# Loads and folded weights at the start of a one-core hybrid kernel: another order on the queues

## The chip, the cores and the metric

The kernel runs on one core of a Trainium2 chip. The metric is the device time of the whole program in microseconds (us). TensorE (PE) multiplies matrices, its weight loads are listed as PEld; VectorE is DVE, ScalarE is ACT, GpSimd is POOL. SP computes nothing here; it issues DMAs. ACT and POOL issue DMAs too. An engine works through its own instructions in order, and an instruction that issues a DMA is one of them.

## What is computed

The reference is three layers on one image of 256 channels and 64 x 64 pixels, which are also seen as 4096 tokens of 256 values; `_gn` is a group norm over groups of 8 channels and all pixels, `_ln_t` a layer norm per token.

```python
x = x + _L0_conv_ref(_gn(x), ...)
t = _to_tokens(x)
t = t + _L1_attn_ref(_ln_t(t), ...)
t = t + _L1_ffn_ref(_ln_t(t), ...)
x = _from_tokens(t, x)
...
# layer 0: 8 heads of 32, boxes of 64, 32 and 16 pixels around each pixel
q, k = sigmoid(einsum(x, Wq)), sigmoid(einsum(x, Wk))
v = v / max(norm(v), 1e-12)
Ik, Ikv = _integral(k), _integral(einsum('bfhw,bghw->bfghw', k, v))
for w in WINDOWS:
    wk, wkv = _box(Ik, Hh // w, Hh, Ww), _box(Ikv, Hh // w, Hh, Ww)
    outs.append(einsum('bdhw,bdfhw->bfhw', q, wkv) / (einsum('bdhw,bdhw->bhw', q, wk)[:, None] + 1e-06))
return einsum('bchw,oc->bohw', concatenate(outs, axis=1), Wout) + bout[None, :, None, None]
...
# layer 1: causal attention over 4096 tokens, then a small MLP
A = softmax(where(causal, einsum('bqd,bkd->bqk', q, k), MASK_FILL) / D ** 0.5)
out = _layernorm(einsum('bqk,bkd->bqd', A, v) + x, g_ln, beta_ln)
return _layernorm(relu(out @ W1.T + b1) @ W2.T + b2, g_lnff, beta_lnff)
...
# layer 2: two of eight experts, chosen from the mean over the tokens
h = gelu(einsum('nd,edf->enf', xf, W1) + b1[:, None, :])
y = einsum('enf,efd->end', h, W2) + b2[:, None, :]
return _layer_norm(einsum('ne,end->nd', w_dense, y) + x, gamma, beta)
```

Layer 1 needs Wq and Wk only as a product. For that the kernel folds them once: mm = Wq^T Wk, a vector mb from Wk and bq, one more column of the value weights from Wq and bk, and one number from bq and bk.

## The kernel before, in words

`conv_attn_hybrid` calls `window_attention` (layer 0), `causal_attention` (layer 1) and `experts` (layer 2). The change touches the start of layer 0 and the order of some DMAs within it.

At the start of `window_attention`, `load(m)` fetches chunk m of x, 1024 pixels, as two DMAs of 512 KB: channels 0 to 127 by SP, 128 to 255 by ACT (L202). All four chunks are asked for at once; the fourth lies in the buffer `vh`, which is not needed until later. ACT then issues six tables of masks (L212). `first(psum)` is `folded` (L716 on): it loads Wq, Wk, bq, bk, Wv, bv on ACT's queue into buffers of its own, transposes Wq and Wk on PE (L736), copies them out on DVE (L737), multiplies (L748, L753, L758, L765), and stores the four results `fold` to DRAM by SP (L771), from where `Causal.load` (L813) gets them back at the end of layer 0. After it, SP is given the 32 loads of the tokens, `t` (L217, 128 KB each), and POOL that of bout (`bo`, L219). POOL loads three slices of layer 0's weights (L305) and Wout (`wo`, L309).

The group norm: DVE takes `bn_stats` of each half of each chunk (16 in all, L261) and two aggregates (L262); PE multiplies the means by `groups` (L264), DVE forms `d2` (L268 to L270), PE multiplies again (L272), ACT takes the square root (L274), DVE the reciprocal (L275).

`window_heads` runs twice, for heads 0 to 3 (`hg` 0) and 4 to 7 (`hg` 1). Its first stage is a loop over four chunks: `normalise(m + 1)` on DVE (L610), `project` (L517: keys, then queries; ACT's sigmoids L520, L522), `values` (L540, copied by ACT L543; at its end SP stores v to DRAM, four DMAs, L558), then at m = 0 everything in the list `late`, `block_sums`, and `turned` (L573). `fetch(m)` brings v back in another order (L565, two DMAs per chunk). For `hg` 1 `normalise` loads its chunk of x anew (L202).

The second stage goes through lists of window parts: `push` fills four PSUM buffers by PE (L349, L358), and ACT and DVE empty them (L327, L329, five of eight on ACT); `add` multiplies with v (L391). Six PSUM buffers turn in a ring. Where a group of columns is complete, `store` has ACT copy the sum (L402) and issue its DMA to DRAM, `oscratch` (L403); later SP brings it back as `ov` (L667). POOL builds running sums and boxes, then adds bout to the tokens (L652). `convolve` (L505) multiplies by Wout and adds to the tokens.

The order of the work: PE and POOL are in the order of the program text inside `window_heads` (`manual_schedule`); the other engines, SP among them, are put in order by a scheduler that works from costs of its own. At the start of `window_attention` PE is scheduled too. The built program keeps eight completion counters for the DMAs that SP and ACT issue, and hands them round from DMA to DMA. A DMA waits, on the engine that issues it, until the one before it on its counter has landed.

Of the kernel before, what the change touches and what calls it, by code (L numbers as in the profile page):

```python
# [152 lines left out]
@with_exitstack  # L153
def conv_attn_hybrid(ctx: ExitStack, tc: tile.TileContext, a, out):
    nc = tc.nc

    const = ctx.enter_context(tc.tile_pool(name="const", bufs=1))
    ident = const.tile([P, P], F32, name="ident")
    make_identity(nc, ident)
    eps5 = const.tile([P, 1], F32, name="eps5")  # L160
    nc.vector.memset(eps5, 1e-5)

    tok = ctx.enter_context(tc.tile_pool(name="tok", bufs=1))
    t = tok.tile([P, NT, D], F32, name="t")

    dram = ctx.enter_context(tc.tile_pool(name="folded", bufs=1, space=bass.MemoryType.DRAM))
    low = ctx.enter_context(tc.tile_pool(name="low", bufs=1))
    iks = ctx.enter_context(tc.tile_pool(name="iks", bufs=1, reuse_waits="tile"))
    causal = Causal(tc, a, t, ident, eps5, low, iks)
    window_attention(tc, a, t, eps5, ident, causal, lambda psum: folded(tc, dram, psum, a, ident))  # L170
    big = ctx.enter_context(tc.tile_pool(name="l12big", bufs=1, reuse_waits="tile"))
    keep = ctx.enter_context(tc.tile_pool(name="l12keep", bufs=1, reuse_waits="tile"))
    given = Given(nc, a, keep, causal)
    x2 = causal_attention(tc, t, ident, eps5, causal, big, given)
    experts(tc, a, t, out, ident, eps5, given, x2)


def window_attention(tc, a, t, eps5, ident, causal, first):
# [5 lines left out]
    with ExitStack() as ctx:  # L184
# [21 lines left out]
        vh = causal.vh  # L206
        raws = [load(m) for m in range(3)]
        raws.append(load(3, vh.rearrange("p j e -> p (j e)")[:, 0:2048].rearrange("p (c n) -> p c n", c=DC)))
        tables = []
        for i, o in enumerate(window_tables()):  # L210
            s = w.tile(list(o.shape), BF16, name=f"table{i}")
            nc.scalar.dma_start(out=s, in_=a[f"mask{i}"])  # L212
# [37 lines left out]
        pt = psum()  # L250
        wide = sm.tile([P, 4, 32], F32, name="wide", bufs=1)
        nc.vector.tensor_copy(wide, sums.unsqueeze(1).to_broadcast([P, 4, 32]))
        nc.tensor.transpose(pt[:, 0:P], wide.rearrange("p w j -> p (w j)"), ident)
        nc.vector.tensor_copy(spreadh, pt[:, 0:P])


        mv = sm.tile([P, DC, 2], F32, name="mv")
        for c in range(DC):
# [3 lines left out]
            nc.vector.bn_aggr(out=mv[:, c, :], in_=st)  # L262
        pm = psum()
        nc.tensor.matmul(pm[:, 0:DC], lhsT=groups, rhs=mv[:, :, 0], start=True, stop=True)  # L264
        gm = w.tile([P, DC], F32, name="gm")
        nc.vector.tensor_copy(gm, pm[:, 0:DC])
        d2 = sm.tile([P, DC], F32, name="d2")
        nc.vector.tensor_sub(d2, mv[:, :, 0], gm)  # L268
        nc.vector.tensor_mul(d2, d2, d2)
        nc.vector.tensor_add(d2, d2, mv[:, :, 1])  # L270
        pv = psum()
        nc.tensor.matmul(pv[:, 0:DC], lhsT=groups, rhs=d2, start=True, stop=True)  # L272
        rs = w.tile([P, DC], F32, name="rs")
        nc.scalar.activation(rs, pv[:, 0:DC], AF.Sqrt, bias=eps5)  # L274
        nc.vector.reciprocal(rs, rs)  # L275
# [19 lines left out]
def window_heads(tc, a, t, ident, hg, norm, raws, load, psum, pools, tables, consts, late, causal):  # L295
# [417 lines left out]
BIG = NT - 20  # L713


def folded(tc, dram, psum, a, ident):  # L716


    nc = tc.nc
    with ExitStack() as tmp:  # L720
        s = tmp.enter_context(tc.tile_pool(name="foldsm", bufs=1, side="right"))
        mm = s.tile([P, DC, D], F32, name="mm")
        mb = s.tile([P, DC], F32, name="mb")
        wvu = s.tile([P, DC, D + 2], F32, name="wvu")
        nc.gpsimd.memset(wvu[:, :, 0:1], 0.0)
        bvc = s.tile([P, D + 2], F32, name="bvc")
        nc.gpsimd.memset(bvc[:, 0:1], 1.0)
        wT = {}
        for name in ("Wq", "Wk"):
            src = s.tile([P, DC, D], F32, name=f"f{name}")  # L730
            nc.scalar.dma_start(out=src, in_=a["L1_" + name].rearrange("(c p) e -> p c e", p=P))
            dst = s.tile([P, DC, D], F32, name=f"t{name}")
            for e in range(DC):
                pt = psum()[:, 0:D]
                for c in range(DC):
                    nc.tensor.transpose(pt[:, c * P : (c + 1) * P], src[:, c, e * P : (e + 1) * P], ident)  # L736
                nc.vector.tensor_copy(dst[:, e, :], pt)  # L737
            wT[name] = dst
        col = {}
        for name in ("bq", "bk"):  # L740
            col[name] = s.tile([P, DC], F32, name=f"f{name}")
            nc.scalar.dma_start(out=col[name], in_=a["L1_" + name].rearrange("(c p) -> p c", p=P))
        nc.scalar.dma_start(out=wvu[:, :, 1 : D + 1], in_=a["L1_Wv"].rearrange("(c p) e -> p c e", p=P))
        nc.scalar.dma_start(out=bvc[:, 1 : D + 1], in_=a["L1_bv"].partition_broadcast(P))
        for c in range(DC):
            pm = psum()[:, 0:D]
            for e in range(DC):
                nc.tensor.matmul(pm, lhsT=wT["Wq"][:, e, c * P : (c + 1) * P], rhs=wT["Wk"][:, e, :],  # L748
                                 start=(e == 0), stop=(e == DC - 1))
            nc.vector.tensor_copy(mm[:, c, :], pm)  # L750
            pb = psum()[:, 0:D]
            for e in range(DC):
                nc.tensor.matmul(pb[:, 0:1], lhsT=wT["Wk"][:, e, c * P : (c + 1) * P], rhs=col["bq"][:, e : e + 1],  # L753
                                 start=(e == 0), stop=(e == DC - 1))
            nc.vector.tensor_copy(mb[:, c : c + 1], pb[:, 0:1])
            pb = psum()[:, 0:D]
            for e in range(DC):
                nc.tensor.matmul(pb[:, 0:1], lhsT=wT["Wq"][:, e, c * P : (c + 1) * P], rhs=col["bk"][:, e : e + 1],  # L758
                                 start=(e == 0), stop=(e == DC - 1))
            nc.vector.tensor_copy(wvu[:, c, D + 1 :], pb[:, 0:1])  # L760
        bqs = s.tile([P, DC, P], F32, name="bqs")
        nc.vector.tensor_copy(bqs, col["bq"].unsqueeze(2).to_broadcast([P, DC, P]))
        pb = psum()[:, 0:D]
        for e in range(DC):
            nc.tensor.matmul(pb[:, 0:1], lhsT=bqs[:, e, :], rhs=col["bk"][:, e : e + 1],  # L765
                             start=(e == 0), stop=(e == DC - 1))
        nc.vector.tensor_copy(bvc[:, D + 1 :], pb[:, 0:1])
        out = []
        for src in (mm, mb, wvu, bvc):
            d = dram.tile(list(src.shape), F32, name=f"fold{len(out)}")  # L770
            nc.sync.dma_start(out=d, in_=src)  # L771
            out.append(d)
    return out


class Causal:
# [554 lines left out]
```

## Time and profile before

| what | value |
|---|---|
| three timed runs, median | 1993.42 us (1993.35 to 1994.79) |
| the profiled execution's own time | 1994.53 us |
| its span | 1992.8 us |
| mean granted TensorE clock | 0.982 |
| PE busy | 1859.6 us (93%), 20326 instructions |
| DVE, ACT, POOL busy | 1000.5, 777.4, 431.8 us |
| DMA over the span | 53.34 MB, mean 27 GB/s |

The busy row of an engine gives one digit for each of 40 equal slices of the span. A line of the order of time gives start, length, engine, source line, operation, output and input, shapes, how many were merged, and in brackets the idle time before it and what ended that. An engine name with a q (SPq, ACTq) is the engine's queue of issues. A line of waits gives who waited, on what, for how long in total, how often, and the longest. The lines themselves stand in the prediction.

### The profile page before, as it was taken

The numbers are of one execution on the slowest core, as the hardware profiler recorded it, in microseconds if no ns is written. First come the engines' busy times: TensorE is split into PE (matmuls) and PEld (weight loads), VectorE is DVE, ScalarE is ACT, GpSimd is POOL, SyncE is SP. The second block draws the span as 40 slices with busy tenths as digits, with TensorE's granted clock in tenths as the row PEclk, the third lists the DMA queues.
The fourth block names the chain that finished last, engine by engine and source line by source line (L and its number), as shares of the span: only waits on it lengthen the run. The fifth ranks groups of instructions, "written<-read, shape, count | busy, mean of one in ns | idle before, by whom it ended". The sixth has DMA issues, their size and how long they took to land.

```text
span 1992.8 us, 46271 instructions
## 1 busy us (share of the span) xinstructions
PE 1859.6 (93%) x20326; PEld 1218.4 (61%) x20326; DVE 1000.5 (50%) x2190; ACT 777.4 (39%) x1331; POOL 431.8 (22%) x709
## 2 busy tenths in 40 slices
PE   4999999999999999999999999999999999879998
PEld 2655565555665555555575656665666666657777
DVE  4644555544554565555663444554553655443343
ACT  1566444444456644444414233233333234223322
POOL 1384323232155123333110000000000000031220
PEclk9999999999999999999999999999999999879999
DMA  7211100000331100000100000000000000010000
GB/s 242 82 52 45 29 13 18 13 18 12 104 92 40 45 18 18 13 13 13 50 2 0 1 0 1 0 1 0 1 0 1 0 1 0 1 43 22 21 22 22
DMA packets 66890, 53.34 MB, mean 27 GB/s; under 512 B 37568, under 2 KB 56792, under 8 KB 66688
## 3 DMA queue, kind: packets, MB, share of 16 engines
q1 hardware_dynamic: 57296, 31.87, 5.8%
q10 hardware_dynamic: 8128, 14.67, 2.1%
q0 software_dynamic: 1264, 3.84, 0.6%
q8 instruction: 159, 2.61, 0.6%
q14 instruction: 43, 0.35, 0.1%
HBM read 32.93 MB, written 17.44 MB: 25 GB/s over the span
## 4 chain that ended last, share of the span: by engine, by line
PE 42%; DVE 6%; ACT 3%; issue 1%; POOL 0%; ACTq 0%; DVEq 0%; POOLq 0%
PE po L1001 11%; PE pa L957 10%; PE ph L1265 6%; PE py L1285 6%; PE pt L987 2%; PE pm L1058 1%; PE acc L391 1%; PE pm L1068 1%; DVE lnst L704 1%; PE ps L505 1%; DVE sT L990 1%; PE ps L358 1%; DVE nbs L965 1%; PE pm L916 1%; ACT s L970 1%
## 5 line engine op out<-in xcount | busy, mean ns | idle before, releaser
L327 ACT ACTIVATE pm<-ps 128x512 f32<-128x512 f32 (+19 forms) x734 | 362.4, 558 | 348.4 <-issue 194.1
L329 DVE TENSOR_SCALAR pm<-ps 128x512 f32<-128x512 f32 (+23 forms) x442 | 267.6, 636 | 315.7 <-PE ps L358 234.5
L391 PE MATMUL acc<-pm,vh 128*32 128x248 f32 (+22 forms) x3424 | 218.5, 356 | 16.8 <-DVE pm L329 16.7
L358 PE MATMUL ps<-q,kh 32*128 32x248 f32 (+23 forms) x3424 | 204.8, 354 | 0.0
L957 PE MATMUL pa<-k,qT 128*128 128x512 f32 (+3 forms) x416 | 180.2, 574 | 7.1 <-ACT qT L918 5.6
L349 PE MATMUL ps<-table,table 32*128 32x192 bf16 (+19 forms) x2512 | 143.1, 261 | 24.4 <-ACT rn L477 8.4
L990 DVE COPY sT<-pt 128x512 f32<-128x512 f32 (+3 forms) x144 | 92.7, 644 | 142.9 <-PE pt L987 142.7
L391 PEld LDWEIGHTS acc<-pm,vh 128*32 128x32 f32 x3424 | 87.3, 110 | 108.5 <-issue 60.8
L349 PEld LDWEIGHTS <-table 32*128 32x128 bf16 x2512 | 50.0, 92 | 162.5 <-issue 155.7
L358 PEld LDWEIGHTS ps<-q,kh 32*128 32x128 f32 x3424 | 142.6, 188 | 7.3 <-issue 2.5
L426 POOL TENSOR_TENSOR y<-y,rn 128x512 f32<-128x512 f32 x32 | 41.3, 1290 | 449.5 <-DVE y L425 297.9
L959 ACT ACTIVATE s<-pa,v 128x512 f32<-128x512 f32 (+3 forms) x112 | 73.8, 661 | 152.1 <-PE pa L957 151.9
L957 PEld LDWEIGHTS pa<-k,qT 128*128 128x128 f32 x416 | 75.7, 191 | 89.3 <-issue 72.4
L965 DVE TENSOR_REDUCE nbs<-s 128x1 f32<-128x512 f32 (+4 forms) x120 | 77.6, 652 | 80.4 <-ACT s L959 59.1
L1285 PE MATMUL py<-w,hT 128*128 128x256 f32 x512 | 111.8, 379 | 0.0
L1001 PE MATMUL po<-kh,sT 128*128 128x257 f32 x406 | 102.8, 395 | 8.7 <-DVE sT L990 8.5
L1285 PEld LDWEIGHTS py<-w,hT 128*128 128x128 f32 x512 | 97.3, 190 | 15.7 <-issue 1.9
L391 PE MATMUL acc<-pm,v 128*32 128x192 f32 (+11 forms) x1600 | 98.5, 360 | 3.9 <-DVE pm L329 2.4
L358 PE MATMUL ps<-q,k 32*128 32x192 f32 (+11 forms) x1600 | 98.4, 359 | 0.0
L1001 PEld LDWEIGHTS po<-kh,sT 128*128 128x128 f32 x406 | 74.7, 195 | 22.4 <-DVE sT L990 13.2
L505 PE MATMUL ps<-l0wo,y 128*128 128x256 f32 x384 | 87.0, 383 | 0.0
L948 POOL MEMSET s<- 128x32 f32 x20 | 2.5, 124 | 376.4 <-PE pt L987 348.4
(304 smaller groups left out, 2899.0 us busy)
## 6 DMA issues: line engine op xcount, KB each, us to landing
oscratch<-ov ACTq DMA_DIRECT2D x32, 256.0 KB
ov<-oscratch SPq DMA_DIRECT2D x32, 256.0 KB
t<-in_xT SPq DMA_DIRECT2D x32, 128.0 KB
vscratch<-v SPq DMA_DIRECT2D x32, 128.0 KB
vh<-vscratch SPq DMA_DIRECT2D x16, 256.0 KB
raw<-in_x SPq DMA_DIRECT2D x7, 512.0 KB
raw<-in_x ACTq DMA_DIRECT2D x7, 512.0 KB
out<-y SPq DMA_DIRECT2D x7, 512.0 KB
```

The costliest lines, as they stand in the source:

```text
L327: nc.scalar.activation(dst, src, AF.Relu)
L329: nc.vector.tensor_scalar_max(dst, src, 0.0)
L349: nc.tensor.matmul(got[h][:, spot].rearrange("p (y x) -> p y x", y=part.r1 - part.r0), lhsT=spread[hs, int(part.vertical), :], rhs=bias[hs ...
L358: nc.tensor.matmul(got[h][:, spot].rearrange("p (y x) -> p y x", y=part.r1 - part.r0), lhsT=keys[hs], rhs=q[hs, part.r0 : part.r1, part.c0 ...
L391: nc.tensor.matmul(out, lhsT=v, rhs=pm[:, h, spot].rearrange("p (y x) -> p y x", y=part.r1 - part.r0), start=fresh, stop=(left[key] == 0), ...
L505: nc.tensor.matmul(pt[:, i * D : (i + 1) * D], lhsT=ys[wi, Y][:, (2 * j + i) * P : (2 * j + i + 1) * P], rhs=wo[:, n, :], start=(n == 0), ...
L957: nc.tensor.matmul(pp[:, 0:m], lhsT=qTs[g][:, c, i * P - g * 512 : n - g * 512], rhs=x[b // 512][c][:, 0:m], start=(c == 0), stop=(c == DC ...
L965: nc.vector.tensor_reduce(nbs[:, at : at + 1], s[:, b : b + m], AX.X, ALU.max)
L990: nc.vector.tensor_copy(sT[:, 0:full], pt[:, 0:full])
L1001: nc.tensor.matmul(acc, lhsT=sT[0:m, j * P : (j + 1) * P], rhs=rhs, start=(b == 0), stop=(m != P))
L1265: nc.tensor.matmul(ph, lhsT=w1v[:, e, c, f, :], rhs=x2[g][c], start=(c == 0), stop=(c == DC - 1))
L1285: nc.tensor.matmul(py, lhsT=hT[:, e, f, j * P : (j + 1) * P], rhs=w2v[:, e, f, :], start=(e + f == 0), stop=(e == 1 and f == FC - 1))
```

## The change: what it does

- The fold becomes a generator in four pieces. Its buffers lie in the space of `t` instead of a pool. Its six loads are issued by ACT right behind x, ahead of the tables.
- A square root of a constant on ACT (`root`) loads the table of that function early.
- `bn_stats` go through the chunks in the order in which they are loaded, both channel halves in turn.
- PE's order at the start is written out: the transposes of Wq and Wk, the norm's first product, the fold's product for c = 0, the norm's second product, the fold's product for c = 1. bk is a further column of the Wk operand, so that a product has 257 columns and needs no narrow one for the value column. The copies out of PSUM go to ACT.
- What is left of the fold (six narrow products, the stores to DRAM) and the transpose for `spreadh` come in `late`, behind the first chunk's values, with the load of bout. The load of Wout follows them.
- SP joins the engines in the order of the text inside `window_heads`. All of `fetch` comes behind the last store of v. The 32 loads of the tokens follow the fetches.

```diff
-    window_attention(tc, a, t, eps5, ident, causal, lambda psum: folded(tc, dram, psum, a, ident))
+    window_attention(tc, a, t, eps5, ident, causal, lambda psum: folded(tc, dram, psum, a, ident, t))
...
+        folding = first(psum)
+        next(folding)
+        root = sm.tile([P, 1], F32, name="root", bufs=1)
+        nc.scalar.activation(root, eps5, AF.Sqrt)
         tables = []
...
-        causal.fold = first(psum)
-        for i in range(NT):
-            nc.sync.dma_start(out=t[:, i, :], in_=a["xT"][i * P : (i + 1) * P, :])
         bo = w.tile([P, D], F32, name="l0bo")
-        nc.gpsimd.dma_start(out=bo, in_=a["L0_bout"].partition_broadcast(P))
...
+        for j in range(NQ):
+            for c in range(DC):
+                nc.vector.bn_stats(out=st[:, c, j, :], in_=raws[j // 2][:, c, (j % 2) * 512 : (j % 2 + 1) * 512])
         for c in range(DC):
-            st = sm.tile([P, NQ, 6], F32, name="st")
-            for j in range(NQ):
-                nc.vector.bn_stats(out=st[:, j, :], in_=raws[j // 2][:, c, (j % 2) * 512 : (j % 2 + 1) * 512])
-            nc.vector.bn_aggr(out=mv[:, c, :], in_=st)
+            nc.vector.bn_aggr(out=mv[:, c, :], in_=st[:, c])
+        with tc.manual_schedule(engines={mybir.EngineType.PE}):
+            next(folding)
+            pm = psum()
+            nc.tensor.matmul(pm[:, 0:DC], lhsT=groups, rhs=mv[:, :, 0], start=True, stop=True)
+            next(folding)
...
+            nc.tensor.matmul(pv[:, 0:DC], lhsT=groups, rhs=d2, start=True, stop=True)
+            rs = w.tile([P, DC], F32, name="rs")
+            nc.scalar.activation(rs, pv[:, 0:DC], AF.Sqrt, bias=eps5)
+            nc.vector.reciprocal(rs, rs)
+            next(folding)
+
+        def rest():
+            pt = psum()
+            nc.tensor.transpose(pt[:, 0:P], wide.rearrange("p w j -> p (w j)"), ident)
+            nc.scalar.copy(spreadh, pt[:, 0:P])
+            causal.fold = next(folding)
+            nc.gpsimd.dma_start(out=bo, in_=a["L0_bout"].partition_broadcast(P))
+
-        late = []
+        late = [rest]
...
-    nc.gpsimd.dma_start(out=wo, in_=a["L0_Wout"].rearrange("(w g p) e -> g p w e", g=2, p=P)[hg])
...
-    with tc.manual_schedule(engines={mybir.EngineType.PE, mybir.EngineType.Pool}), ExitStack() as keys:
+    ordered = {mybir.EngineType.PE, mybir.EngineType.Pool, mybir.EngineType.SP}
+    with tc.manual_schedule(engines=ordered), ExitStack() as keys:
...
                 if m == 0:
                     while late:
                         late.pop(0)()
+                    nc.gpsimd.dma_start(out=wo, in_=a["L0_Wout"].rearrange("(w g p) e -> g p w e", g=2, p=P)[hg])
...
             for m in range(4):
                 fetch(m)
+            if hg == 0:
+                for i in range(NT):
+                    nc.sync.dma_start(out=t[:, i, :], in_=a["xT"][i * P : (i + 1) * P, :])
```

The new `folded`, from its loads on (`take` hands out pieces of `t`):

```python
    for name in ("Wq", "Wk"):
        nc.scalar.dma_start(out=src[name], in_=a["L1_" + name].rearrange("(c p) e -> p c e", p=P))
    for name in ("q", "k"):
        nc.scalar.dma_start(out=wT["W" + name][:, :, D], in_=a["L1_b" + name].rearrange("(c p) -> p c", p=P))
    nc.scalar.dma_start(out=wvu[:, :, 1 : D + 1], in_=a["L1_Wv"].rearrange("(c p) e -> p c e", p=P))
    nc.scalar.dma_start(out=bvc[:, 1 : D + 1], in_=a["L1_bv"].partition_broadcast(P))
    yield
    for name in ("Wq", "Wk"):
        for e in range(DC):
            pt = psum()[:, 0:D]
            for c in range(DC):
                nc.tensor.transpose(pt[:, c * P : (c + 1) * P], src[name][:, c, e * P : (e + 1) * P], ident)
            nc.scalar.copy(wT[name][:, e, 0:D], pt)
    yield
    for c in range(DC):
        pm = psum()
        for e in range(DC):
            nc.tensor.matmul(pm[:, 0 : D + 1], lhsT=wT["Wq"][:, e, c * P : (c + 1) * P], rhs=wT["Wk"][:, e, :],
                             start=(e == 0), stop=(e == DC - 1))
        nc.scalar.copy(mm[:, c, :], pm[:, 0:D])
        nc.scalar.copy(wvu[:, c, D + 1 :], pm[:, D : D + 1])
        yield
    nc.vector.tensor_copy(bqs, wT["Wq"][:, :, D : D + 1].to_broadcast([P, DC, P]))
    pb = psum()
    for c in range(DC):
        for e in range(DC):
            nc.tensor.matmul(pb[:, c : c + 1], lhsT=wT["Wk"][:, e, c * P : (c + 1) * P], rhs=wT["Wq"][:, e, D : D + 1],
                             start=(e == 0), stop=(e == DC - 1))
    for e in range(DC):
        nc.tensor.matmul(pb[:, DC : DC + 1], lhsT=bqs[:, e, :], rhs=wT["Wk"][:, e, D : D + 1],
                         start=(e == 0), stop=(e == DC - 1))
    nc.vector.tensor_copy(mb, pb[:, 0:DC])
    nc.vector.tensor_copy(bvc[:, D + 1 :], pb[:, DC : DC + 1])
    out = []
    for s in (mm, mb, wvu, bvc):
        d = dram.tile(list(s.shape), F32, name=f"fold{len(out)}")
        nc.sync.dma_start(out=d, in_=s)
        out.append(d)
    yield out
```

More of the change, by code (lines that the diff above doesn't have):

```diff
@@ L249, in window_attention @@
         spreadh = w.tile([P, P], F32, name="spreadh")
-        pt = psum()
         wide = sm.tile([P, 4, 32], F32, name="wide", bufs=1)
         nc.vector.tensor_copy(wide, sums.unsqueeze(1).to_broadcast([P, 4, 32]))
-        nc.tensor.transpose(pt[:, 0:P], wide.rearrange("p w j -> p (w j)"), ident)
-        nc.vector.tensor_copy(spreadh, pt[:, 0:P])
         mv = sm.tile([P, DC, 2], F32, name="mv")
+        st = sm.tile([P, DC, NQ, 6], F32, name="st", bufs=1)
+        for j in range(NQ):
+            for c in range(DC):
+                nc.vector.bn_stats(out=st[:, c, j, :], in_=raws[j // 2][:, c, (j % 2) * 512 : (j % 2 + 1) * 512])
@@ L258, in window_attention @@
         for c in range(DC):
-            st = sm.tile([P, NQ, 6], F32, name="st")
-            for j in range(NQ):
-                nc.vector.bn_stats(out=st[:, j, :], in_=raws[j // 2][:, c, (j % 2) * 512 : (j % 2 + 1) * 512])
[L262 to L275, printed above, removed]
+            nc.vector.bn_aggr(out=mv[:, c, :], in_=st[:, c])
[4 more added lines that the diff above has]
+            next(folding)
+            gm = w.tile([P, DC], F32, name="gm")
+            nc.vector.tensor_copy(gm, pm[:, 0:DC])
+            d2 = sm.tile([P, DC], F32, name="d2")
+            nc.vector.tensor_sub(d2, mv[:, :, 0], gm)
+            nc.vector.tensor_mul(d2, d2, d2)
+            nc.vector.tensor_add(d2, d2, mv[:, :, 1])
+            pv = psum()
+            nc.tensor.matmul(pv[:, 0:DC], lhsT=groups, rhs=d2, start=True, stop=True)
[3 more added lines that the diff above has]
+            next(folding)
@@ L713, with folded @@
 BIG = NT - 20
-def folded(tc, dram, psum, a, ident):
+def folded(tc, dram, psum, a, ident, t):
     nc = tc.nc
[L720 to L763, printed above, removed]
-        for e in range(DC):
-            nc.tensor.matmul(pb[:, 0:1], lhsT=bqs[:, e, :], rhs=col["bk"][:, e : e + 1],
-                             start=(e == 0), stop=(e == DC - 1))
[L767 to L773, printed above, removed]
@@ new lines, in folded, with take @@
+    flat, at = t.rearrange("p i d -> p (i d)"), [0]
+    def take(*shape):
+        n = int(np.prod(shape))
+        s = flat[:, at[0] : at[0] + n]
+        at[0] += n
+        return s.rearrange("p (c e) -> p c e", c=shape[0]) if len(shape) == 2 else s
+    mm, mb, wvu, bvc = take(DC, D), take(DC), take(DC, D + 2), take(D + 2)
+    nc.gpsimd.memset(wvu[:, :, 0:1], 0.0)
+    nc.gpsimd.memset(bvc[:, 0:1], 1.0)
+    src = {name: take(DC, D) for name in ("Wq", "Wk")}
+    wT = {name: take(DC, D + 1) for name in ("Wq", "Wk")}
@@ new lines, in folded @@
+    bqs = take(DC, P)
+    for name in ("Wq", "Wk"):
+        nc.scalar.dma_start(out=src[name], in_=a["L1_" + name].rearrange("(c p) e -> p c e", p=P))
+    for name in ("q", "k"):
+        nc.scalar.dma_start(out=wT["W" + name][:, :, D], in_=a["L1_b" + name].rearrange("(c p) -> p c", p=P))
+    nc.scalar.dma_start(out=wvu[:, :, 1 : D + 1], in_=a["L1_Wv"].rearrange("(c p) e -> p c e", p=P))
+    nc.scalar.dma_start(out=bvc[:, 1 : D + 1], in_=a["L1_bv"].partition_broadcast(P))
+    yield
+    for name in ("Wq", "Wk"):
+        for e in range(DC):
+            pt = psum()[:, 0:D]
+            for c in range(DC):
+                nc.tensor.transpose(pt[:, c * P : (c + 1) * P], src[name][:, c, e * P : (e + 1) * P], ident)
+            nc.scalar.copy(wT[name][:, e, 0:D], pt)
@@ new lines, in folded @@
+    yield
+    for c in range(DC):
+        pm = psum()
+        for e in range(DC):
+            nc.tensor.matmul(pm[:, 0 : D + 1], lhsT=wT["Wq"][:, e, c * P : (c + 1) * P], rhs=wT["Wk"][:, e, :],
+                             start=(e == 0), stop=(e == DC - 1))
+        nc.scalar.copy(mm[:, c, :], pm[:, 0:D])
[3 more added lines that the diff above has]
+    pb = psum()
+    for c in range(DC):
+        for e in range(DC):
+            nc.tensor.matmul(pb[:, c : c + 1], lhsT=wT["Wk"][:, e, c * P : (c + 1) * P], rhs=wT["Wq"][:, e, D : D + 1],
+                             start=(e == 0), stop=(e == DC - 1))
@@ L776 @@
+    for e in range(DC):
+        nc.tensor.matmul(pb[:, DC : DC + 1], lhsT=bqs[:, e, :], rhs=wT["Wk"][:, e, D : D + 1],
+                         start=(e == 0), stop=(e == DC - 1))
+    nc.vector.tensor_copy(mb, pb[:, 0:DC])
+    nc.vector.tensor_copy(bvc[:, D + 1 :], pb[:, DC : DC + 1])
+    out = []
+    for s in (mm, mb, wvu, bvc):
+        d = dram.tile(list(s.shape), F32, name=f"fold{len(out)}")
+        nc.sync.dma_start(out=d, in_=s)
+        out.append(d)
+    yield out
 class Causal:
```

## The prediction, before the run

> **What bounds the kernel now.** I read the page's slices first, then who waited for whom on PE and ACT in the first 45 us, then the order of time of the first 45 us, and last the same view around the three places at which the change moves a DMA.
>
> ```profile
> PE   4999999999999999999999999999999999879998
> DMA  7211100000331100000100000000000000010000
> ```
> A slice is 49.8 us. PE is full from the second slice on; only the first shows a large hole, and there the DMA engines are at 70%. So whatever PE gains in the first 40 us ends the kernel earlier by as much, unless later waits eat it.
>
> ```profile
> PE ps L736 <- DMA fWq<-in_L_Wq: 26.2, 1, 26.2
> PE ps L517 <- DVE kh L610: 1.3, 1, 1.3
> ```
> Waits of PE in 0:45 (total, times, longest): one wait of 26.2 us, for the weights that are folded, not for x.
>
> ```profile
> 6.08 14.81 ACTq L212 DMA_DIRECT2D table<-in_mask  x6
> ...
> 21.75 0.39 ACTq L731 DMA_DIRECT2D fWq<-in_L_Wq  x1
> ...
> 23.36 0.37 DVE L262 BATCH_NORM_AGGREGATE mv<-st 128x2 f32<-128x48 f32 x1
> ...
> 26.19 1.09 PE L736 MATMUL ps<-ident,fWq 128*128 128x128 f32 x4 [26.19 <-DMA fWq<-in_L_Wq]
> ...
> 36.77 0.43 PE L264 MATMUL ps<-mv,groups 128*128 128x2 f32 x2
> ...
> 39.95 5.31 PE L517 MATMUL ps<-kh,l0Wk 128*128 128x512 f32 x8 [1.33 <-DVE kh L610]
> ```
> Order of time: start, length. ACT issues Wq only at 21.75, after six tables. The statistics are complete at 23.73 (23.36 + 0.37), but their first product, L264, stands behind the whole fold on PE and runs at 36.77. The projections, the work that then never stops, begin at 39.95.
>
> [...] between 10 and 20 us the DMA share is 1.03 at 369 GB/s, for SP, ACT and POOL together. [...] ACT's table load of L274, which needs no data, stands still until 27.97, when ACT's last issue (27.57 + 0.37) is over. [...] the first projection matmuls take up to 1222 ns, later ones 592; the first k is ready 3.4 us after the start, the second 1.7 us later.
>
> The built programs' waits add what the code doesn't say: DMAs from SP and ACT take turns on eight completion counters, and each waits, on the engine that issues it, until the DMA before it on its counter has landed. That is why the tables and Wq were late: they waited for token loads on SP.
>
> **Part 1, the start (gain).** By the trace's landings the four SP halves of x land at 5.88, 10.42, 14.56, 18.03, the ACT halves up to 18.47. POOL's loads beside them are 0.90 MB (bout, three weights, Wout); 0.51 MB of it goes, at 369 GB/s 1.4 us; some 0.2 MB of tokens and tables that slipped in at the end goes too, 0.5 us. I put the last halves at 16.2 and 16.7. POOL's three weights stay: "nothing beside it" is not quite so.
> Statistics: four bn_stats after the last half, 4 x 0.64 = 2.55, two aggregates 0.65: 19.9. Before, they ended at 23.73.
> Fold: Wq and Wk follow x in ACT's queue, 256 KB each, about 0.75 us at the same rate: landed about 17.5 and 18.2. Transposes 2 x 1.1: 19.3. ACT's evacuations stand behind its table issues, the last two of which wait for bq and bk: about 19.4. Four copies at 0.36 to 0.4 (an ACT copy of 128x256 takes 0.358): 21.0. The product for the mean (L264 before), now right behind the transposes, runs at 19.9; d2 follows 1.2 later (36.77 to 37.98 before), 21.1.
> The fold's first product now stands ahead of the variance product: 2.1 us at the cold rate (L748: 2.08), 21.0 to 23.1. Then the variance product; ACT has two evacuations (0.55) ahead of the square root, which ends about 24.2; reciprocal and normalise as before (38.95 to 39.95) give 25.2. The second fold product, 23.7 to 25.8, ends last. **Projections start at 25.9 instead of 39.95: 14.0 us** (12 to 16: weights 2 us later, or x 1.5 us earlier). [...]
>
> **Part 2, what is put behind the first values (loss).** A transpose and 6 narrow products, 12 records at the 0.117 us of a warm 128x128 one (32 in 3.73), on a PE without holes: **1.6 us** (1.4 to 3, if cold). Two more PSUM buffers of six are hidden by ACT's v copies, which are 1.2 us behind PE.
>
> **Part 3, tokens behind the fetches (loss).** Times here are those of before; all lie about 13.2 earlier after.
>
> ```profile
> 94.51 3.20 SPq L558 DMA_DIRECT2D vscratch<-v  x4
> 100.17 1.71 SPq L565 DMA_DIRECT2D vh<-vscratch  x2
> ```
> ```profile
> 101.64 0.58 ACT L402 COPY ov<-acc 128x512 f32<-128x512 f32 x1
> 102.25 0.35 ACTq L403 DMA_DIRECT2D oscratch<-ov  x1
> 102.79 1.57 ACT L327 ACTIVATE pm<-ps 128x512 f32<-128x512 f32 x3 [0.57 <-PE ps L358]
> ...
> 109.18 0.33 ACTq L403 DMA_DIRECT2D oscratch<-ov  x1
> ```
> SP's order is now written out: all eight fetches follow the last store of v (landed 101.5), then 32 token loads. In the built program ACT's first oscratch store takes its counter after the 4th token load, the second after the 25th. Eight fetches are 2 MB: at 350 to 400 GB/s behind the stores until about 105.4; four token loads at 0.3 to 0.4 each and 0.9 to land: about 107.5. ACT would want to issue at 102.25, so it stands 5.2 us. Behind it wait the PSUM evacuations L327; PE has less than a push of free PSUM, some 0.5 us: loss 4.7. Load 25 lands 21 x 0.38 later, 115.5; the second store would come at 109.18 + 4.7 = 113.9: 1.6, loss 0.8. [...] **Sum 6.3 us.** No such wait is in the trace, so from both sides: 2 if the fetches were done by the time of the stores (the last fetch can't be issued before 101.5), 10 if each load takes 0.42 and the fetches queue fully.
> At nothing: POOL's bias add needs tokens at 148.9, 30 us after they land; bout and Wout likewise (first used at 148.9 and 238.2), POOL being idle when it issues them. ov's loads come at 204, long after the 32 issues.
>
> **Part 4, SP's written order in the second half of the heads (loss).**
>
> ```profile
> 544.56 0.33 SPq L202 DMA_DIRECT2D raw<-in_x  x1
> 549.59 2.76 SPq L558 DMA_DIRECT2D vscratch<-v  x4
> ```
> The last chunk of x now goes behind the four stores of v: issued at 552.4, landed 1.2 after the last of them (555.2, the distance that the chunk before shows): 556.4. PE wants it at 557.41, but DVE now has two scans (2.38) between its halves: the second half at about 560.5, wanted at 559.1: **1.5 us** (0 to 4). Fold loads for the next stage go from 946.84 to about 977.5, behind ov's last loads; 13 issues take 7 us, first use is at 1009: nothing, 25 us of cover. Square-root table and the four copies moved to ACT: in waits of the start, counted above.
>
> **Sum.** -14.0 - 0.8 + 1.6 + 6.3 + 1.5 = -5.4 us. The profiled execution's own time is 1994.53 (span 1992.8 and 1.7 around it), so 1989.1; it is 1.1 over the median, against which I predict 1993.4 - 5.4 = **1988.0**.
>
> **Rivals.** (a) The stores find their counters free: the fetches of the first three chunks run before, so loss 1 or 2 in part 3: -10 to -12, about 1982. For it: 350 GB/s of DMA with nothing else to do; against: SP is in order and the last store of v lands at 101.5. (b) The start gives less, since PE's order ties the norm to the fold's weights: bq and bk land 2 us later[...]: about -1, 1992.5; it counts as no change. (c) Slower: ACT's stalls. Each of the 32 token loads takes 0.8 instead of 0.38[...], so load 4 lands at 110, load 25 at 127: stalls of 7.5 and 10[...]; with parts 2 and 4 that is 25 against 14.8: about 2003.7. It decides from 0.6 us per load on. Against: before, token loads landed every 0.3 us around 43. (d) That the change does nothing at the start is excluded by the built order: the mean's product follows 8 transposes only.
>
> **Chances.** Forecast case 45% (1985 to 1990.5), (a) 25% (1979 to 1985), (b) 21% (1990 to 1996), (c) 9%. About 0.2%, 4 us, is what a measurement can tell from no change. Faster by more (below 1989.4): all of (a) and 38 of the 45: 0.63. Within: the rest of the forecast and (b): 0.28. Slower: 0.09. Range 1980.5 to 1995: it leaves out the ends of (a) and all of (c).
>
> **What would show it.** Right: first projection at 24 to 28 us; ACT waiting twice for DMA t in 85 to 105 us, with PE holes behind it; a DVE wait for raw near 540. Wrong: no ACT wait there (then about 1982); a start above 30; or ACT stalls above 12 us in sum (then no gain).

## The result, and the profile after it

| | before | after |
|---|---|---|
| median of 20 runs each, on one chip | 1994.32 us (1989.57 to 2000.17) | 1989.88 us (1984.08 to 1995.43) |
| ratio after / before, 95% interval | | 0.9975 (0.9965 to 0.9985) |
| span of the profiled execution | 1992.8 us | 1988.4 us |
| mean granted TensorE clock | 0.982 | 0.979 |

The change gains 4.4 us (3 to 7 by the interval), 5.4 were forecast. The sum was nearly right, but three of its terms were not: the start gained 2.8 us more, the stores cost 4.4 more, and the 1.5 put on SP's order did not come that way. That these errors nearly cancel is luck.

The slices of the changed kernel's page, PE and DMA:

```profile
PE   6899999999999999999999999999999999879998
DMA  5421100000330110000200000000000000010000
```

The first slice went from 4 to 6: less hole at the start. The second went from 9 to 8: a new hole. Order of time of PE at the start (start, length, what ran, in brackets the idle time before it):

```profile
15.98 1.94 PE L762 MATMUL ps<-ident,t 128*128 128x128 f32 x8 [15.98 <-DMA t<-in_L_Wq]
18.05 0.56 PE L265 MATMUL ps<-mv,groups 128*128 128x2 f32 x2
19.09 2.08 PE L768 MATMUL ps<-t 128*128 128x257 f32 x4 [0.48 <-ACT t L763]
20.97 0.42 PE L274 MATMUL ps<-d,groups 128*128 128x2 f32 x2
21.25 2.06 PE L768 MATMUL ps<-t 128*128 128x257 f32 x4
23.11 4.63 PE L527 MATMUL ps<-kh,l0Wk 128*128 128x512 f32 x8
```

The wait for Wq ends at 15.98 instead of 26.19, the mean's product runs at 18.05 instead of 36.77, and the projections start at 23.11 instead of 39.95. Now the place of the first store of `oscratch`, again in order of time:

```profile
85.62 0.58 ACT L412 COPY ov<-acc 128x512 f32<-128x512 f32 x1 [0.85 <-PE acc L401]
...
93.73 0.34 ACTq L413 DMA_DIRECT2D oscratch<-ov  x1
94.18 1.08 ACT L337 ACTIVATE pm<-ps 128x512 f32<-128x512 f32 x2 [7.97 <-DMA t<-in_xT]
94.83 0.31 PE L359 MATMUL ps<-table,table 32*128 32x192 bf16 x1 [6.89 <-ACT pm L337]
```

ACT has the sum copied at 86.20, but issues its store only at 93.73, 0.07 after the fourth token load has landed (93.66), and the PSUM copies L337 stand behind it, put down to a token load. PE stands for 6.89. The eight counters show at the start of the same trace: SP and ACT have issued eight DMAs by 2.94, and the ninth, Wq, goes at 6.03, when ACT's first has landed (6.01). The stretches around it (busy times of PE, its weight loads, DVE, ACT and POOL, then the granted clock, the DMA share and GB/s):

```profile
85.00:90.00 5.00, 2.94 (x57) 1.46 (x47) 1.08 (x2) 0.58 (x1) 4.53 (x7) 1.00 1.00 314
90.00:100.30 10.30, 5.30 (x54) 2.95 (x57) 1.29 (x2) 2.66 (x5) 8.58 (x24) 0.50 0.94 313
100.30:113.00 12.70, 11.93 (x215) 6.84 (x211) 4.45 (x7) 7.59 (x15) 10.20 (x33) 1.00 0.52 165
```

In the middle one the clock is at half for 10.24 us, and PE's 5.30 us of work there would have taken about 2.65 at full rate (an estimate: half the time at twice the clock; the 16 products of L368 take 2.04 here at 95.56 and 1.08 in e1 at 87.75).

**A ruler for what follows.** The programs have the same work in the same order after the start, so the start of one instruction in two traces can be subtracted. The table gives that difference against the trace of before (negative is earlier). It separates places, which a total of 1990 us can't.

| place (time before) | after | e1 | e2 | e3 | e4 | e5 | e6 | e8 | e10 | e11 |
|---|---|---|---|---|---|---|---|---|---|---|
| first key copy (43.6) | -17.5 | -18.4 | -18.0 | -17.2 | -18.3 | -10.5 | -4.0 | -18.1 | -17.2 | -16.1 |
| v of the last chunk (87.2) | -15.9 | -16.2 | -15.9 | -14.2 | -16.0 | -7.3 | -4.0 | -13.1 | -15.6 | -14.2 |
| third `ov` copy (113.0) | -5.3 | -16.3 | -6.4 | -12.5 | -4.0 | -7.4 | -4.1 | -13.2 | -15.6 | -14.3 |
| 16th `ov` copy (204.3) | -5.2 | -16.2 | -6.2 | -12.4 | -3.9 | -7.4 | -4.0 | -13.0 | -15.6 | -14.3 |
| late in layer 1 (1708) | -4.4 | -13.1 | -8.7 | -13.8 | -2.5 | -8.1 | -4.0 | -15.6 | -15.7 | -16.7 |

From the fourth row to the fifth the shifts drift by up to 3 us, both ways. Most of it sits at short stretches of half clock, mostly 3.4 us long, which lie elsewhere in each trace: between 200 and 1400 us they sum to 30.7 us in before, 34.1 in after, 37.5 in e1, 23.9 in e8. So the upper four rows are read for causes, and totals 1 or 2 us apart are not.

### The profile page after: what moved, and what is told of

Same layout as the page of the kernel before. It is cut to its first block, busy times and chain, and to the rows that moved or that the text cites. A ratio compares the mean times of both kernels' runs of the same rounds, so it can differ in the third digit from the quotient of the medians.

```text
span 1988.4 us, 46248 instructions
## 1 busy us (share of the span) xinstructions
PE 1859.1 (93%) x20318; PEld 1217.5 (61%) x20318; DVE 997.7 (50%) x2180; ACT 779.9 (39%) x1341; POOL 431.4 (22%) x709
## 3 DMA queue, kind: packets, MB, share of 16 engines
q8 instruction: 159, 2.61, 0.5%
## 4 chain that ended last, share of the span: by engine, by line
PE 43%; DVE 6%; ACT 3%; issue 1%; POOL 0%; ACTq 0%; POOLq 0%; DVEq 0%
PE po L1017 11%; PE pa L973 10%; PE ph L1281 6%; PE py L1301 6%; PE pt L1003 2%; PE pm L1074 1%; PE acc L401 1%; PE pm L1084 1%; DVE lnst L719 1%; PE ps L515 1%; DVE sT L1006 1%; PE ps L368 1%; DVE nbs L981 1%; PE pm L932 1%; ACT s L986 1%
## 5 line engine op out<-in xcount | busy, mean ns | idle before, releaser
L337 ACT ACTIVATE pm<-ps 128x512 f32<-128x512 f32 (+19 forms) x734 | 362.4, 558 | 357.9 <-issue 190.4
L401 PE MATMUL acc<-pm,vh 128*32 128x248 f32 (+22 forms) x3424 | 218.5, 356 | 16.9 <-DVE pm L339 16.7
L368 PE MATMUL ps<-q,kh 32*128 32x248 f32 (+23 forms) x3424 | 205.0, 354 | 0.0
L368 PEld LDWEIGHTS ps<-q,kh 32*128 32x128 f32 x3424 | 142.9, 188 | 7.1 <-issue 2.3
L1301 PEld LDWEIGHTS py<-w,hT 128*128 128x128 f32 x512 | 97.3, 190 | 15.7 <-issue 1.9
L368 PE MATMUL ps<-q,k 32*128 32x192 f32 (+11 forms) x1600 | 100.3, 362 | 0.5 <-issue 0.5
```

The costliest lines, as they stand in the source:

```text
L337: nc.scalar.activation(dst, src, AF.Relu)
L368: nc.tensor.matmul(got[h][:, spot].rearrange("p (y x) -> p y x", y=part.r1 - part.r0), lhsT=keys[hs], rhs=q[hs, part.r0 : part.r1, part.c0 ...
L401: nc.tensor.matmul(out, lhsT=v, rhs=pm[:, h, spot].rearrange("p (y x) -> p y x", y=part.r1 - part.r0), start=fresh, stop=(left[key] == 0), ...
L1301: nc.tensor.matmul(py, lhsT=hT[:, e, f, j * P : (j + 1) * P], rhs=w2v[:, e, f, :], start=(e + f == 0), stop=(e == 1 and f == FC - 1))
```

## The experiments

Ratios are against the kernel before, on the same chip, with 95% intervals.

**e1: tokens early.** The 32 loads move to behind the fold's stores.

```diff
                     while late:
                         late.pop(0)()
+                    if hg == 0:
+                        for i in range(NT):
+                            nc.sync.dma_start(out=t[:, i, :], in_=a["xT"][i * P : (i + 1) * P, :])
...
-            if hg == 0:
-                for i in range(NT):
-                    nc.sync.dma_start(out=t[:, i, :], in_=a["xT"][i * P : (i + 1) * P, :])
```

> The 32 token loads are issued by SP behind the fold's stores at the first chunk, not behind the eight fetches. Theory (the first oscratch store stands on ACT until the token load before it on its completion counter has landed): its counter now belongs to the first fetch, which landed at 86.2 in the changed kernel, so it issues by 86.5 instead of 93.7; no ACT wait for t, no halved clock near 90, the shift of the third ov copy against before stays at -15 to -16 instead of -5.3, and the time is 1978 to 1981 (ratio 0.992 to 0.9935). Rival (the loss comes from the traffic of fetches and tokens itself, or from the stage being early): the eight fetches still run at 82 to 92, so half or more of the loss stays: 1984 to 1988.

Measured: 1979.63 us, 0.9921 (0.9906 to 0.9936). The same place in e1:

```profile
85.30 0.59 ACT L412 COPY ov<-acc 128x512 f32<-128x512 f32 x1 [0.87 <-PE acc L401]
85.97 0.34 ACTq L413 DMA_DIRECT2D oscratch<-ov  x1
86.46 1.57 ACT L337 ACTIVATE pm<-ps 128x512 f32<-128x512 f32 x3 [0.57 <-PE ps L368]
```

The store follows its copy, there is no half clock before 494 us, and the shift stays at -16.3. The eight fetches still run there, so they alone don't cost it. It is among the fastest versions found; e3, e8, e10 and e11 below can't be told from it by their totals.

**e2: fetches back in the loop.**

```diff
-            for m in range(4):
-                fetch(m)
+                for n in ((), (), (0, 1), (2,))[m]:
+                    fetch(n)
+            fetch(3)
```

> The fetches of chunks 0 to 2 are back in the loop (0 and 1 behind the third chunk's stores, 2 behind the fourth's), the tokens stay last. The first oscratch store now takes its counter from the tenth token load. Theory: fetch 3 can't be issued before the last store of v has landed (85.6), tokens follow every 0.35 us from about 87.3, the tenth lands near 91, so ACT stands about 5 us instead of 8, PE about 4 instead of 6.9: 2.5 to 4 us better than the changed kernel, 1985.5 to 1988. Rival (the queue of eight fetches is the cause): six of eight fetches are gone from in front of the store, so the stall goes almost wholly: about 1980.

Measured: 1986.5 us, 0.9956 (0.9941 to 0.9971).

```profile
85.60 0.59 ACT L412 COPY ov<-acc 128x512 f32<-128x512 f32 x1
...
94.38 0.34 ACTq L413 DMA_DIRECT2D oscratch<-ov  x1
94.82 1.57 ACT L337 ACTIVATE pm<-ps 128x512 f32<-128x512 f32 x3 [8.63 <-DMA t<-in_xT]
95.47 0.31 PE L359 MATMUL ps<-table,table 32*128 32x192 bf16 x1 [7.55 <-ACT pm L337]
```

With fewer fetches in front, ACT stood longer, 8.63. By the trace's landings the tenth token load landed at 94.30, and the store was issued at 94.38. So the counter decides and the rival fell; my landing time of 91 was wrong, since the last fetch landed at 89.49, not 87, and ten loads took 4.8. The total is in the range, but the mechanism gives only 1.0 of it at the third copy; the rest is drift.

**e3: the same bytes in four loads.**

```diff
-                for i in range(NT):
-                    nc.sync.dma_start(out=t[:, i, :], in_=a["xT"][i * P : (i + 1) * P, :])
+                for i in range(0, NT, 8):
+                    nc.sync.dma_start(out=t[:, i : i + 8, :],
+                                      in_=a["xT"][i * P : (i + 8) * P, :].rearrange("(i p) d -> p i d", p=P))
```

> The same 4 MB of tokens at the same place, in four loads of 1 MB instead of 32. The first store's counter now belongs to the third fetch (landed at 88.9 in the changed kernel), the second's to the sixth (92.3, wanted at about 98). Theory: ACT stands 2.5 us at the first store and not at the second; PE loses about 2; no halved clock; 1980.5 to 1983.5. Rival (traffic): same bytes at the same time, so the loss stays: 1988 to 1991.

Measured: 1980.51 us, 0.9929 (0.9912 to 0.9946).

```profile
87.37 0.59 ACT L412 COPY ov<-acc 128x512 f32<-128x512 f32 x1
...
89.82 0.34 ACTq L413 DMA_DIRECT2D oscratch<-ov  x1
90.25 1.57 ACT L337 ACTIVATE pm<-ps 128x512 f32<-128x512 f32 x3 [2.30 <-DMA vh<-vscratch]
90.90 0.24 PE L359 MATMUL ps<-table,table 32*128 32x192 bf16 x1 [1.22 <-ACT pm L337]
```

The wait is for a fetch, as the counters say, 2.30 long; PE lost 1.7 in all (-14.2 to -12.5), and the clock stayed full there. Same 4 MB, same place: traffic is not the cause.

**e4: SP left to the scheduler for heads 4 to 7.**

```diff
     ordered = {mybir.EngineType.PE, mybir.EngineType.Pool, mybir.EngineType.SP}
+    if hg:
+        ordered.remove(mybir.EngineType.SP)
```

> SP is left to the scheduler for heads 4 to 7, as before the change; the rest is the changed kernel. Theory: the last chunk of x is asked for ahead of the second chunk's stores again, DVE's wait for it goes, and the shift near 560 stays at -7.0 instead of falling to -5.3 to -5.9: 1.0 to 1.5 us better than the changed kernel. Rival (the later loss is the place of the clock's short dips alone): no difference, within 0.3.

Measured: 1992.07 us, 0.9988 (0.9979 to 0.9997). A miss. The last chunk of x was asked for early again and DVE's second half came 6.2 earlier than in before, with PE's shift then at -5.4; yet the shift still fell there, from -5.44 to -4.15. Waits between 535 and 560, first in after, then in e4:

```profile
DVE kh L621 <- DMA raw<-in_x: 5.6, 3, 2.4
PE ps L583 <- issue: 1.0, 1, 1.0
```
```profile
DVE kh L623 <- DMA raw<-in_x: 2.3, 2, 1.5
PE ps L583 <- issue: 1.1, 1, 1.1
```

DVE's wait halves, PE's hole is the same, and it is "issue": PE waited for nothing that the profile shows. SP's order was not the cause. The 1.3 us by which e4 lies behind the changed kernel at 113 us are from heads 0 to 3, which the edit doesn't touch: its store went at 94.79 instead of 93.73.

**e5: 17 token loads beside x** (the rows of `t` that the fold leaves free), on the base of e1.

```diff
+        for i in range(15, NT):
+            nc.sync.dma_start(out=t[:, i, :], in_=a["xT"][i * P : (i + 1) * P, :])
         bo = w.tile([P, D], F32, name="l0bo")
...
-                        for i in range(NT):
+                        for i in range(15):
```

> As the version with the tokens behind the fold's stores, but 17 of the 32 token loads (the rows of t that the fold doesn't use) are issued by SP right behind x. Theory (a token load beside x's tail and the fold's weights costs by its bytes and by its completion counters, which ACT's loads of bk, Wv, bv and the tables then wait for, with ACT's copies of the transposes behind them): 17 loads are 2.2 MB, 6 us at 369 GB/s, so ACT's table issues end 3 to 5 us later than 18.15 and the projections start at 26 to 28 instead of 23.2: 3 to 5 us slower than that version, 1982.5 to 1985. Rival (what counts is only that the fold's loads stand ahead of the tables): no difference, within 0.5 of its 1979.6.

Measured: 1986.94 us, 0.9969 (0.9955 to 0.9984).

```profile
17.05 1.94 PE L764 MATMUL ps<-ident,t 128*128 128x128 f32 x8 [17.05 <-DMA t<-in_L_Wq]
...
20.91 4.93 ACTq L216 DMA_DIRECT2D table<-in_mask  x5
25.89 1.20 ACT L765 COPY t<-ps 128x256 f32<-128x256 f32 x4 [5.97 <-DMA table<-in_mask]
26.86 2.08 PE L770 MATMUL ps<-t 128*128 128x257 f32 x4 [7.66 <-ACT t L765]
...
30.87 3.85 PE L529 MATMUL ps<-kh,l0Wk 128*128 128x512 f32 x8
```

The start is 7.7 later than in e1 (23.18), more than expected. Wq comes 1.0 later (17.05, e1 16.05) and x not at all: the statistics of its last chunk begin at 15.06 and 15.02. The rest is ACT, which stands in its table issues until 25.84 while the finished transposes of Wq and Wk wait to be copied.

**e11: as e5, and the tables issued by SP behind those tokens.**

```diff
-            nc.scalar.dma_start(out=s, in_=a[f"mask{i}"])
+            nc.sync.dma_start(out=s, in_=a[f"mask{i}"])
```

> As the version with 17 token loads beside x, and the six tables are issued by SP behind those tokens instead of by ACT. The bytes beside x are the same; no table issue of ACT waits for a token's counter any more. Theory (of the 7.7 us that the tokens beside x cost at the start, the bytes are 1 and the counters 6 to 7): ACT's copies come at 19.9 instead of 25.9, the projections start at 24.5 to 25.5 instead of 30.9, 5.5 to 6.5 faster than that version. Rival (the bytes delay the fold's loads and x): start stays at 29 or later.

Measured: 1979.01 us, 0.9929 (0.9910 to 0.9948).

```profile
19.73 1.18 ACT L765 COPY t<-ps 128x256 f32<-128x256 f32 x4
20.68 2.08 PE L770 MATMUL ps<-t 128*128 128x257 f32 x4 [1.53 <-ACT t L765]
...
24.70 4.46 PE L529 MATMUL ps<-kh,l0Wk 128*128 128x512 f32 x8
```

As expected: 6.2 of the 7.7 return with the same bytes beside x. That no token load stands between ACT and its copies is worth 6 us; "nothing beside x" is worth about the other 1.5, its bytes and its turns on the counters together.

**e10: as e1, and the tables on SP.**

> As the version with the tokens behind the fold's stores, and the six tables of masks are issued by SP instead of ACT. Theory: ACT's copies of the transposes, which stood behind the table issues until 18.2, follow the transposes from 16.9 on, so the fold's product for c = 0 runs right behind the mean's product at 18.6 instead of 19.2 and the projections start at 22.4 to 22.8 instead of 23.2; the clock gives nothing more: 0.4 to 0.8 faster than that version where the stages begin, too little for the timed runs to tell. Rival: [...] x lands 0.5 to 1 us later, and the start stays at 23 or goes to 24.

Measured: 1980.73 us, 0.9942 (0.9923 to 0.9961). The edit is the line of e11. A miss, on the rival's side, though not by its reason: the statistics of x ended as in e1, but Wq came at 17.14 instead of 16.05, and ACT's own loads were issued later, since the tables had changed whose turn it was on which counter: Wk at 9.21 instead of 6.55, bk at 15.01 instead of 9.96, bv at 17.81 instead of 13.22. ACT's table load and its copies stand behind them: copies at 19.59 instead of 18.19, projections at 24.45 instead of 23.18. So 1.3 us go here with 1.1 MB of tables and no token beside x, about as much as e11 loses with 2.2 MB of tokens: the loss doesn't follow the bytes.

**e6: before, with one part of the change:** the fold's loads ahead of the tables.

```diff
+        causal.fold = first(psum)
         tables = []
...
-        causal.fold = first(psum)
```

> The kernel before with one thing of the change: the fold's six loads are issued by ACT ahead of the six tables. Theory (the start's gain is made of the early weights and of the new order on PE): the transposes start near 19 to 20 instead of 26.2, the fold on PE takes its 10.6 us as before, the mean's product follows it at about 30 and the projections start at 32.5 to 34: 6 to 7.5 us of the 16.8, time 1986 to 1988. Rival (the place of the fold's loads in ACT's queue is everything): projections at 23 to 26, 1978 to 1981. Other rival (the order on PE is everything): projections near 40, 1993.

Measured: 1990.4 us, 0.9983 (0.9972 to 0.9995).

```profile
20.14 1.09 PE L736 MATMUL ps<-ident,fWq 128*128 128x128 f32 x4 [20.14 <-DMA fWq<-in_L_Wq]
...
30.91 1.28 DVE L261 BATCH_NORM_STATS2 st<-vh 128x6 f32<-128x512 f32 x2
32.22 0.37 DVE L262 BATCH_NORM_AGGREGATE mv<-st 128x2 f32<-128x48 f32 x1
32.73 0.56 PE L264 MATMUL ps<-mv,groups 128*128 128x2 f32 x2 [2.07 <-DVE mv L262]
...
36.03 5.22 PE L517 MATMUL ps<-kh,l0Wk 128*128 128x512 f32 x8 [1.32 <-DVE kh L610]
```

The weights came 6 us earlier, the start only 3.9 (36.03). All three expectations missed: the fold's copies now stood on DVE between the statistics, which ended at 32.59 instead of 23.73, and PE waited 2.07 for them. So the early loads alone bring 3.9 of the 16.8; the rest comes with what the change does beside them, above all the copies on ACT, the statistics as x arrives and PE's written order. No run separates these.

**e8: both fold products behind the first values**, on the base of e1.

```diff
             nc.tensor.matmul(pm[:, 0:DC], lhsT=groups, rhs=mv[:, :, 0], start=True, stop=True)
-            next(folding)
...
             nc.vector.reciprocal(rs, rs)
-            next(folding)
...
+            for _ in range(DC):
+                next(folding)
             causal.fold = next(folding)
```

> As the version with the tokens behind the fold's stores, but both products of the fold (L768) stand behind the first chunk's values, so that the norm's two products follow one another. Theory: the variance product comes at 19.5 instead of 21.0, the projections start at about 21.4 instead of 23.2; [...] the two products cost 2.1 at full rate where they now lie: 0.5 to 1.5 slower than that version's 1979.6. Rival (the products delay the norm and nothing else): 1.5 to 2 faster.

Measured: 1978.18 us, 0.9922 (0.9910 to 0.9935), in the total not to be told from e1. By place it loses. The projections of the keys start at 21.65, 1.5 earlier, but those of the queries at 28.12 instead of 26.64: the projection matmuls follow one another every 0.85 us until 27.7 and every 0.43 only then, while in e1 they run at 0.43 from 23.6 on. Then the two products cost their time behind the values. At the last chunk it is 3.1 behind e1 (-13.1 against -16.2), more than expected; of the 0.5 to 1.5 put, 0.6 was an estimate for slower projections. In e1 the two products run between the norm's steps, where PE would else be idle, and the projections behind them start at full pace.

**e9: twenty more products of one column**, added to the changed kernel behind the first values. Their output is read by nobody.

```diff
+            pad = psum()
+            for i in range(20):
+                nc.tensor.matmul(pad[:, i : i + 1], lhsT=groups, rhs=ident[:, i : i + 1], start=True, stop=True)
```

> The changed kernel with twenty more products of one column on PE behind the first chunk's values, into a buffer that nobody reads. They move the place in PE's program at which a block of its instructions ends. Theory (the 1.0 us in which PE waits for nothing the profile shows, in the third chunk's transposes of heads 4 to 7, is the arrival of such a block, 1.4 us ahead of which a 16 KB instruction fetch ends in five traces): the hole is gone or lies elsewhere, and the fetch lies 1.5 to 2.5 us earlier against PE's work. Rival (the hole comes from SP's order or from DVE): it stays at L583, 0.9 to 1.1 us. The twenty products themselves cost 1.2 to 2.5 us near 36.

Measured: one run, 2000.87 us. Two lines of PE, the padding and the place of the hole:

```profile
33.42 6.24 PE L286 MATMUL ps<-ident,groups 128*128 128x1 f32 x40
```
```profile
562.41 1.09 PE L586 MATMUL ps<-ident,k 128*128 128x128 f32 x8
563.63 3.67 PE L530 MATMUL ps<-kh,l0Wk 128*128 128x512 f32 x8
```

The hole in the third chunk's transposes is gone: eight in a row in 1.09. The last 16 KB instruction fetch before them ends at 553.58, 8.8 us ahead, where in after one ends 0.1 ahead; 1.5 to 2.5 us earlier was expected. Other holes of this kind moved too (2.0 before a product of L597 at 583, 0.9 at 58). With the hole gone another wait shows: the projections lose 0.35 (the shift goes from 5.94 to 6.29), since their first one, at 563.63, waits for DVE's first part of x's late half, which ends at 563.48. The padding took 6.2, far over my 1.2 to 2.5, and the clock went to half for 10.2 us at 35.9, in the midst of it: the records come every 0.11 us before, every 0.21 after.

## Why the prediction was right, and where it was not

**The start, -14.0 forecast, -16.8 measured (too small).** The steps ran in the order given, each 1.8 to 2.8 early. The terms that were off most are the landings: statistics of x's last chunk could begin at 14.94 (16.2 to 16.7 put), and Wq was there at 15.98 (17.5). For x I had taken off 1.9 us of bytes, and 3.1 went. Tokens beside x are not the reason: the same statistics begin at 15.06 in e5 and 15.01 in e11, with 17 token loads beside x, but at 18.13 in e6, which keeps bout and Wout on POOL's queue, against 18.05 in before. So it goes with these two loads, 0.51 MB, at more than the 1.4 put for their bytes; no run moved them alone. **The first key tile, -0.8 forecast, -0.7 measured.** The 0.8 was an estimate: half of the 1.7 by which the first tile's products took longer than the second's in before (3.43 against 1.72). Those of the first tile start 0.7 to 1.0 us apart there, those of the second 0.43. In after the first tile takes 2.75 and the second 1.71, so the first key copy is 17.5 early.

**Behind the values, +1.6.** Measured +1.4 between the first chunk's values and the second chunk's (the shift goes from -17.5 to -16.1) and another 0.25 in the third. Right.

**The stores, +6.3 forecast, +10.7 measured, over the upper bound of 10.** (The shift goes from -16.0 at the first `ov` copy to -5.3 at the third.) The mechanism was right; e1, e2 and e3 show it from three sides. Mis-sized were two terms. ACT's store went 7.5 us after its copy, 5.2 were put: the eighth fetch landed at 92.26, 6.7 us after the last store of v (85.58), where I had 3.9; four token loads then took 1.4, where I had 2.1. The 3.9 was too short as a sum already, for 2 MB at the 350 to 400 GB/s put are 5.2 to 6.0 us, and the DMA engines moved 313. PE's hole was 6.9 instead of 4.7. The clock: the last 0.8 in the sum of 6.3 was an estimate, an even chance of one half-clock stretch of 3.4 us, as before has one at 94.4; that a wait on PE brings one was not shown. It was half for 10.24, three times as long, from 2 us into the hole to 5.4 after its end, when PE went on: 2.65. The second store fits: 1.0 against 0.8.

**SP's order in the second half, +1.5.** Here the term fails, though a loss of about that size is there. DVE's last half of x did come late, 5.4 us against PE's shift. But the two scans that I put between its landing and DVE's work on it were over before it landed (at 547.78, landed 550.17), so it came at 550.19, which is 557.2 in the times of before, not 560.5. In after PE doesn't wait for it, since its own hole holds it until then; in e9, without that hole, the wait shows and costs 0.35. The loss of 1.1 near 550 is PE's own hole of 1.0, and e4 keeps it with SP's order undone. The page of after lists fetches of instructions:

```profile
q8 instruction: 159, 2.61, 0.5%
```

159 fetches and 2.61 MB are 16.4 KB each. In all nine traces with the hole (after, e1 to e5, e8, e10, e11) such a fetch ends 1.25 to 1.45 us before PE goes on (in after at 549.35, and PE goes on at 550.75); in e9, with the place shifted, the hole is gone, and before and e6, with the old program, have none there. Before has one of 1.5 at 578 instead, 1.5 us behind such a fetch, where after has 0.35: part of the loss comes back. That the fetch is the cause is supported by this, not proven: no run here changed the fetch alone.

**At nothing.** POOL's loads, `ov`'s loads and the fold's loads: no wait for them appears on PE. Right.

**What is left of the 4.4.** Near 204 us the shift is -5.2, at the end -4.4: 1.9 gained between 270 and 530, where before had three half-clock stretches (306, 350, 514) and after two (387, 506), 0.9 net lost between 550 and 580 (the hole at 550, a half-clock stretch of after at 568, and before's own hole at 578), and 1.7 lost in all between 640 and 773, mostly where after has a stretch at 759 that before has not. The prediction had no term for these.

**The rivals.** (a), the stores find their counters free, was what e1 makes of the kernel: 1979.6, better than the 1982 put, since the start gained more. (c), slower, was wrong in its trigger: token loads landed every 0.35 us, not 0.8; but of its cost the stall of 7.5 was real, and so was a halved clock, for which 5 of its 25 us stood as an estimate (10.24 us at half, about 2.65).

## What to carry to other kernels

Ahead of moving a batch of loads, list for every later DMA which earlier one holds its completion counter, on all the engines that share the counters: here a store on a compute engine inherited the landing time of a load on another queue (store 93.73, load 93.66), and everything behind it on its engine inherited it too. Fewer, larger loads, or loads a stage earlier, cost nothing here and returned 9 (e3) or all (e1) of the 10.7 us. After the waits of 6.9, 7.6 and 8.1 us on PE (after, e2, e4) the 16 products of L368 took 2.04 us, after that of 1.2 (e3) 1.08, so count slower work behind a long wait as well; and compare places in two traces, since totals drift by 2 or 3 us where the code is the same.

## What was not expected of the hardware

- In e9 the granted clock fell to half while PE worked through products of one column (40 records) without a gap (6.10 of 6.10 us busy, second column below): 2.5 us after they began, for 10.2 us. It is one trace, and the cause was not shown. At full clock the records followed one another every 0.11 us, as the transposes of 128 columns do in after (L583, 0.11).

```profile
33.40:39.50 6.10, 6.10 (x42) 6.10 (x41) 2.29 (x4) 0.75 (x2) 2.44 (x4) 0.71 0.38 89
```

- Between 85 and 100 us the DMA engines were full (share 1.00, 0.94) at 313 GB/s, below the 369 GB/s that the start of before showed at a share of 1.03: fetches and tokens took longer than bytes over that rate.
